# A two-stage state-space scan: new start, seven swapped steps of 32 instead of eight, and a new order of the steps that prepare each chunk

## The chip, the core and the metric

The kernel runs on one core of a Trainium2 chip. The metric is the device time of one execution in microseconds, from the median of the runs. A core has five engines with a queue each: TensorE (PE, its weight loads PEld), VectorE (DVE), ScalarE (ACT), GpSimd (POOL) and SyncE (SP), which here only issues DMAs. Each executes its queue in order and waits on semaphores where an input is not there or an output's buffer is not free.

## The reference

Two layers on x of shape (1, 64, 256, 128) in float32. The first is a pair of bidirectional state-space blocks, one along time (stage 0 below), one along frequency (stage 1); the second is a convolutional LSTM. The change is in the first:

```python
def _mamba(u, p):                       # u: sequences x L x 64, d_inner 128, 16 states
    x, z = split(u @ in_proj)           # after an RMS norm of u
    x = silu(causal_conv4(x) + conv_b)
    dt, B, C = split(x @ x_proj)        # 4 + 16 + 16
    dt = softplus(dt @ dt_proj + dt_b)
    h[t] = exp(dt[t] * A) * h[t-1] + dt[t] * B[t] * x[t]      # A = -exp(A_log)
    y[t] = sum over states(h[t] * C[t]) + x * D
    return (y * silu(z)) @ out_proj
```

Each of the two stages runs it forwards and backwards (d = 0, 1) with weights of its own, adds the input, and multiplies by a closing matrix.

## The kernel before

A chunk is 512 tokens (sequences of one stage laid side by side); a stage has 64 chunks. In a chunk each direction d takes 8 steps, so a chunk has 16 steps, and `Stage.run` goes over S = 0 to 1023 in each stage. What a "turn" S of its loop issues, in this order:

- `times_b(S+1)`: bx times B, 1024 elements a partition, on VectorE in PSUM; for a **swapped** step (S % 32 in `SWAPPED`) on GpSimd instead, on a copy in SBUF.
- `recur(S)`: the scan on VectorE. Every eighth turn (S % 8 == 2) `gate` follows on VectorE, and `skip` on ScalarE.
- `outputs(S-1)`: h times C on GpSimd.
- `inputs(S+2)`: TensorE spreads dt*x over the states into one of three PSUM buffers of bx. The buffer is free when `recur(S-1)` is done.
- `decays(S+2)`: ScalarE makes exp(dt*A), two activations that need the tile rep (dt spread over the partitions by a DMA). For a swapped step ScalarE first copies bx to SBUF and writes the decays into its PSUM place. In turn 5 of a chunk two steps' decays are issued, in turn 6 none.
- the head steps of this turn, then in odd turns `add_up(S-2)` on TensorE, in turns 2 and 3 `close_a`, `close_b` and `keep`, then the head steps of S + 0.5.

The head steps prepare the next chunk. The table `HEAD` gives the turn of each, counted from the start of the chunk before; a turn of 16 or more lies in the chunk itself, a negative one in the chunk before that. The names: `load` (DMA of u), `squares`, `means`, `rms`, `normalise` (xn on GpSimd, then four DMAs), `project_x`, `project_z`, `silus` (two table loads and four activations on ScalarE), `project_bc` (pb on TensorE, the copy bc on ScalarE, a DMA to DRAM called away), `softplus_a` (pv on TensorE, three activations), `softplus_b` (three activations), `softplus_sum` (six matmuls, the copy dt on ScalarE), `dt_away` (four DMAs, called there), `times_x` (dtx on GpSimd), `spread_bc` (the DMAs of B and C from away), `spread_dt` (the DMA of a rep of 512 KB from there; rep n of direction d is for step 8d + n, with seven buffers). The order of the table is the order of each queue, SP's too. The small matmuls of the head (px, pz, pv, pb, po, pm) share one PSUM bank, called mm.

`SECOND` is the table for chunk 0, whose first half is written out in `first`. In stage 0, `first` also makes the weights from raw arrays: `shifts`, `gates`, `dt`, `spreads`, `folds`, `residual`, `closing`, mostly on VectorE. The lines of before that the text names: L322 squares, L332 and L333 rms, L351 normalise_here, L360/L361/L364 projections, L398 pv, L419 softplus_sum, L423 dt, L430 there, L441 pb, L443 bc, L445 away, L451 B and C, L460 rep, L553 inputs, L570 a swapped step's copy, L573/L576 decays, L585 a swapped step's product, L588 times_b, L598 the scan, L611 outputs, L620 add_up, L632 skip, L636 gate.

Of the kernel before, what the change touches and what calls it, by code (L numbers as in the profile page):

```python
# [29 lines left out]
F32 = mybir.dt.float32  # L30
# [6 lines left out]
P = 128  # L37
C = 64
# [8 lines left out]
NTOK = 512  # L47
# [12 lines left out]
RESPOND = 6  # L60
NH = 5
LAG = 2
SWAPPED = (2, 5, 9, 14, 18, 21, 25, 30)
EXP_AND_LN = "natural_log_exp_and_others"
SILU = "silu_and_others"
EDGES = (0, 1, LF - 2, LF - 1)
# [2 lines left out]

HEAD = (  # L70
    (-13, "load"),
    (-8.5, "squares"),
    (-4.5, "means"),
    (-4.5, "rms"),
    (-3, "normalise"),
    (0, "project_x", 0),
    (1.5, "project_z", 0),
    (4, "project_z", 1),
    (5, "project_x", 1),
    (5, "silus"),  # L80
    (7.5, "project_bc", 0),
    (8, "softplus_a", 0),
    (8.5, "softplus_b", 0),
    (8.5, "spread_bc", 0, 0),
    (10.5, "softplus_sum", 0),
    (10.5, "dt_away", 0),
    (11.5, "times_x", 0),
    (12, "spread_bc", 0, 1),
    (12, "spread_dt", 0, 0),
    (12, "spread_dt", 0, 1),  # L90
    (12.5, "project_bc", 1),
    (12.5, "spread_dt", 0, 2),
    (13, "softplus_a", 1),
    (13, "softplus_b", 1),
    (13.5, "spread_dt", 0, 3),
    (14.5, "spread_dt", 0, 4),
    (15, "softplus_sum", 1),
    (15.5, "dt_away", 1),
    (16, "spread_dt", 0, 5),
    (16.5, "spread_dt", 0, 6),  # L100
    (16.5, "spread_dt", 0, 7),
    (17, "spread_dt", 1, 0),
    (17.5, "spread_bc", 1, 0),
    (19, "spread_dt", 1, 1),
    (20.5, "times_x", 1),
    (21, "spread_dt", 1, 2),
    (22, "spread_dt", 1, 3),
    (23, "spread_bc", 1, 1),
    (23, "spread_dt", 1, 4),
    (24, "spread_dt", 1, 5),  # L110
    (26.5, "spread_dt", 1, 6),
    (26.5, "spread_dt", 1, 7),
)


# [3 lines left out]
) + (  # L119
    (14, "softplus_a", 1),  # L120
    (15, "softplus_b", 1),
    (15, "softplus_sum", 1),
    (15, "dt_away", 1),
    (16, "spread_bc", 1, 0),
    (16, "spread_bc", 1, 1),
    (17, "times_x", 1),
)

# [1 line left out]
class Mamba:  # L130
# [3 lines left out]
    def __init__(self, ctx, tc, cols, room, d):  # L134
        nc = tc.nc
        self.nc, self.tc, self.d, self.cols = nc, tc, d, cols
        cp = ctx.enter_context(tc.tile_pool(name="m_const", bufs=1))
        self.ident = cp.tile([P, P], F32, name="ident")
        self.mask = cp.tile([P, 2, NK, DL], F32, name="mask")
        self.sel = cp.tile([P, 2, NK, P], F32, name="sel")  # L140
        self.fold = cp.tile([P, NK, 32], F32, name="fold")
        self.ones = cp.tile([P, P], F32, name="ones")
        self.eps = cp.tile([P, 1], F32, name="eps")
        self.Wbc = cp.tile([P, 4, NBC], F32, name="wbc")
        self.cb, self.dtb, self.dp = (cols[:, 4 * n : 4 * n + 4] for n in range(3))
        self.A = cols[:, 12 : 12 + 4 * NG].rearrange("p (i g) -> p i g", i=4)
        self.G1, self.G2, self.Wz, self.Wdt, self.W2, self.W3 = ([] for _ in range(6))
        for i in range(4):
            for n, t, rows, width in (
                ("g1", self.G1, P, P),  # L150
                ("g2", self.G2, P, P),
                ("wz", self.Wz, C, P),
                ("wdt", self.Wdt, P, P),
                ("w2", self.W2, P, C),
            ):
                t.append(cp.tile([rows, width], F32, name=f"{n}{i}", tag=f"{n}{i}"))
        for i in range(2):
            self.W3.append(cp.tile([P, 2, C], F32, name=f"w3{i}", tag=f"w3{i}"))
        b = cp.tile([C, 2], F32, name="lin_b")
        self.b = b  # L160
        self.lin_b = [b[:, i : i + 1] for i in range(2)]

        room = room.rearrange("p t f -> p (t f)")
        at = 0

        def take(rows, *shape):
            nonlocal at
            n = int(np.prod(shape))
            t = room[0:rows, at : at + n]
            at += n  # L170
            return t

        self.win = take(C, 4, 2 * P + 1).rearrange("p (i n) -> p i n", i=4)
        self.cw = take(C, 4, 4, P).rearrange("p (i k n) -> p i k n", i=4, k=4)
        self.xdt = take(RANK, 8, P).rearrange("p (i n) -> p i n", i=8)
        self.ow = take(C, 4, P).rearrange("p (i n) -> p i n", i=4)
        self.lin = take(C, 4, C).rearrange("p (i n) -> p i n", i=4)


        nc.vector.memset(self.ones, 0.0)  # L180
        for h in range(2):
            own = slice(h * C, (h + 1) * C)
            nc.vector.memset(self.ones[own, own], 1.0 / C)
        nc.vector.memset(self.eps, RMS_EPS)
        for w3 in self.W3:
            nc.vector.memset(w3, 0.0)
        make_identity(nc, self.ident)

    def load(self, first):
        dma, d = self.nc.sync.dma_start, self.d  # L190
# [24 lines left out]
        self.nc.scalar.activation(self.A, self.A, AF.Exp)  # L215
        self.nc.vector.tensor_scalar(self.A, self.A, -1.0, None, ALU.mult)

    def dt(self, i, ps):
        self.nc.tensor.matmul(ps[:, 0:P], lhsT=self.xdt[:, i], rhs=self.xdt[:, 4 + i], start=True, stop=True)
        self.nc.vector.tensor_copy(self.Wdt[i], ps[:, 0:P])  # L220

    def gates(self, i):
        self.nc.vector.tensor_copy(self.Wz[i], self.win[:, i, P : 2 * P])
# [26 lines left out]
        nc.vector.tensor_add(w3[0:C, 0], w3[0:C, 0], self.ident[0:C, 0:C])  # L250
        nc.vector.tensor_copy(w3[C:P, 1], w3[0:C, 0])

    def closing(self, i, ps):
        self.nc.tensor.matmul(ps[:, 0:C], lhsT=self.ow[:, i], rhs=self.lin[:, i], start=True, stop=True)
        self.nc.vector.tensor_copy(self.W2[i], ps[:, 0:C])


class Stage:
# [206 lines left out]
    def head(self, ch):  # L465
        todo = {}
        for slot, name, *args in HEAD if ch else SECOND:
            todo.setdefault(slot, []).append((getattr(self, name), (ch, *args)))
        return todo

    def first(self):


        nc, m = self.nc, self.m
        s, time = 2 * self.stage, self.time
        banks = [self.ps_bx.tile([P, 2, NTOK], F32, name="bx", tag="bx") for _ in range(3)]
        self.load(0)
        if time:
            m.load(True)
        self.squares(0)  # L480
        if time:
            m.shifts(0)
        self.means(0)
        self.rms(0)
        nc.scalar.preload_act_table_set(SILU)
        self.normalise_here()
        if time:
            m.dt(0, self.mm("pw"))
            m.load(False)
        x, z = {}, {}  # L490
        for d in range(2):
            x[d] = self.wk.tile([P, NTOK], F32, name="xs", tag="xs", bufs=3)
            z[d] = self.wk.tile([P, NTOK], F32, name="zs", tag="zs", bufs=4)
            self.at["xs", 0, d], self.at["zs", 0, d] = x[d], z[d]
        self.shifted(banks[0][:, 0], s)
        nc.scalar.activation(x[0], banks[0][:, 0], AF.Silu, bias=m.cb[:, s : s + 1])
        nc.scalar.preload_act_table_set(EXP_AND_LN)
        self.softplus_a(0, 0)
        if time:
            m.decay()  # L500
            m.spreads()
            m.gates(0)
            m.shifts(1)
            m.gates(1)
        self.softplus_b(0, 0)
        self.spare = [banks[0][:, 1]]
        self.project_bc(0, 0)
        self.spread_bc(0, 0, 0)
        self.softplus_sum(0, 0)
        self.dt_away(0, 0)  # L510
        self.times_x(0, 0)
        for n in range(4):
            self.spread_dt(0, 0, n)
            if n == 0:
                self.spread_bc(0, 0, 1)
        if time:
            m.dt(1, self.mm("pw"))
        self.shifted(banks[1][:, 0], s + 1)
        for d in range(2):
            self.gated(banks[1 + d][:, 1], s + d)  # L520
        nc.scalar.preload_act_table_set(SILU)
        nc.scalar.activation(x[1], banks[1][:, 0], AF.Silu, bias=m.cb[:, s + 1 : s + 2])
        for d in range(2):
            nc.scalar.activation(z[d], banks[1 + d][:, 1], AF.Silu)
        nc.scalar.preload_act_table_set(EXP_AND_LN)
        self.spare = [banks[2][:, 0]]
        self.project_bc(0, 1)
        if time:
            m.folds(self.mm("pf"))
            for i in (2, 3):  # L530
                m.shifts(i)
                m.gates(i)
                m.dt(i, self.mm("pw"))
            for n in range(2):
                m.residual(n)
            for i in range(4):
                m.closing(i, self.mm("pc"))

# [15 lines left out]
    def swapped(self, S):  # L556


        return S % 32 in SWAPPED

# [125 lines left out]
    def run(self):  # L686
        nch = NCH
        last = 16 * nch
        silu = next(slot for slot, name, *_ in HEAD if name == "silus")
        steps = {}  # L690
# [1 line left out]
            for slot, todo in self.head(ch).items():  # L692
                steps.setdefault(16 * (ch - 1) + slot, []).extend(todo)
        self.first()
        for S in range(int(min(steps)), last + LAG + 4):
            if 0 <= S + 1 < last:
                self.times_b(S + 1)
            if 0 <= S < last:
# [24 lines left out]
            if not self.time and S > 16:  # L723
# [5 lines left out]
                n = S // 16 - 1  # L729
# [533 lines left out]
```

## Time and profile before

| | |
|---|---|
| median of 3 runs | 7323.06 us (7319.82 to 7334.2) |
| the profiled execution | 7325.76 us, span 7324.0 us |
| first to last scan of stage 0 | 48.69 to 3319.25 us |
| first to last scan of stage 1 | 3356.72 to 6629.66 us |
| the LSTM and what prepares it | the rest of the span |
| mean granted TensorE clock | 0.975 |

In the profile an instruction has the line of its kernel, the engine, the operation, and the tiles out<-in. A group's columns are the busy time, the mean of one in ns, and the idle time of its engine just before them with what ended it. In a timeline a line has its start and length in us, and in brackets the idle time before it. Times are from the span's start; the median of the runs and the profiled execution are different executions.

### The profile page before, as it was taken

Reading aid. Unit: us, or ns where it says so; the run is one execution under the profiler, and the core shown is the slowest. Engines: PE = TensorE matmul, PEld = TensorE weight load, DVE = VectorE, ACT = ScalarE, POOL = GpSimd, SP = SyncE. Lnnn points to the kernel's source line nnn. Section 1 sums busy time; section 2 is a strip of 40 time slices with the busy share of each in tenths; the row PEclk is TensorE's granted clock in tenths of the full one; section 3 lists DMA queues with packets and bytes.
Section 4 is the critical chain, followed back from the end, with each engine's and each line's share of the span. In section 5 each row is a group of like instructions: output and inputs, shape, how many; then the busy total and the mean of one; then the engine's idle time right before and its main releaser. Section 6 shows DMA issues by size and latency. Waiting matters only on the chain. (4 is left out here: it accounts for less than half of the span.)

```text
span 7324.0 us, 86482 instructions
## 1 busy us (share of the span) xinstructions
PE 6510.4 (89%) x25104; PEld 2254.8 (31%) x25104; DVE 6924.8 (95%) x4684; ACT 6119.2 (84%) x11092; POOL 6703.3 (92%) x3410
## 2 busy tenths in 40 slices
PE   8888888888888888887898898888888888888999
PEld 2222222222222222222222222222222222226887
DVE  7999999999999999997999999999999999996887
ACT  7888889888898888987999999988998989983333
POOL 6999999999999999997999999999999999995554
PEclk9999999999999999999999999999999999999999
DMA  7888888888888888886888888878888788882000
GB/s 171 206 206 208 199 210 204 205 207 205 210 203 209 206 204 207 204 210 159 208 211 209 210 215 200 208 197 202 206 201 204 199 209 198 205 202 62 15 15 17
DMA packets 505887, 1359.47 MB, mean 186 GB/s; under 512 B 72772, under 2 KB 129732, under 8 KB 505416
## 3 DMA queue, kind: packets, MB, share of 16 engines
q1 hardware_dynamic: 505416, 1353.93, 74.6%
q8 instruction: 205, 3.36, 0.2%
q14 instruction: 266, 2.18, 0.1%
HBM read 1228.34 MB, written 92.27 MB: 180 GB/s over the span
## 5 line engine op out<-in xcount | busy, mean ns | idle before, releaser
L611 POOL TENSOR_TENSOR h<-h,C 128x1024 f32<-128x1024 f32 x2048 | 4797.5, 2366 | 32.4 <-DVE h L598 22.0
L598 DVE TENSOR_TENSOR_SCAN h<-dA,bx 128x1024 f32<-128x1024 f32 x1536 | 3443.8, 2269 | 0.0
L553 PE MATMUL bx<-dtx,sel 64*128 64x512 f32 x8192 | 2578.7, 653 | 364.8 <-DVE h L598 362.5
L588 DVE TENSOR_TENSOR bx<-bx,B 128x1024 f32<-128x1024 f32 x1536 | 1863.7, 1213 | 178.8 <-PE bx L553 178.2
L576 ACT ACTIVATE dA<-rep,cols 128x510 f32<-128x510 f32 (+1 forms) x3072 | 2021.7, 710 | 11.3 <-DMA rep<-there 11.3
L585 POOL TENSOR_TENSOR dA<-dA,B 128x1024 f32<-128x1024 f32 x512 | 1205.9, 2355 | 161.9 <-ACT dA L570 155.8
L553 PEld LDWEIGHTS bx<-dtx,sel 64*128 64x128 f32 x8192 | 733.3, 190 | 1888.1 <-issue 1070.5
L620 PE MATMUL y<-h,fold 128*32 128x512 f32 x8192 | 1239.5, 618 | 12.6 <-POOL h L611 10.9
L598 DVE TENSOR_TENSOR_SCAN h<-bx,dA 128x1024 f32<-128x1024 f32 x512 | 1167.9, 2281 | 15.4 <-POOL dA L585 15.4
L570 ACT COPY dA<-bx 128x1024 f32<-128x1024 f32 x512 | 518.5, 1013 | 352.7 <-PE bx L553 338.0
L576 ACT ACTIVATE bx<-rep,cols 128x510 f32<-128x510 f32 (+1 forms) x1024 | 705.5, 689 | 33.7 <-ACT bx L573 0.4
L398 PE MATMUL pv<-xs,wdt 128*128 128x512 f32 x512 | 341.2, 753 | 261.5 <-ACT bc L443 167.5
L620 PEld LDWEIGHTS y<-h,fold 128*32 128x32 f32 x8192 | 188.5, 109 | 933.5 <-issue 504.0
L435 POOL TENSOR_TENSOR dtx<-dt,xs 128x512 f32<-128x512 f32 x256 | 327.6, 1280 | 54.2 <-ACT dt L423 33.7
L364 PE MATMUL pz<-unp,wz 64*128 64x512 f32 x504 | 283.5, 642 | 91.0 <-ACT X L669 54.0
L360 PE MATMUL px<-unp,g 128*128 128x512 f32 x504 | 283.8, 644 | 9.5 <-DMA unp<-xn 7.0
L419 PE MATMUL pv<-e,ident 128*128 128x512 f32 x512 | 288.1, 645 | 3.4 <-ACT e L402 3.4
L441 PE MATMUL pb<-xs,wbc 128*32 128x512 f32 x504 | 260.9, 599 | 15.6 <-ACT made L809 15.6
L419 PE MATMUL pv<-w,ident 128*128 128x512 f32 x512 | 262.6, 594 | 6.1 <-ACT w L411 6.1
L419 PE MATMUL pv<-lw,ident 128*128 128x512 f32 x512 | 262.3, 594 | 0.0
L361 PE MATMUL px<-unp,g 128*128 128x512 f32 x504 | 257.8, 592 | 0.0
L1150 POOL TENSOR_TENSOR y<-v,X 128x512 f32<-128x512 f32 x32 | 40.6, 1270 | 230.7 <-DVE v L1148 230.7
(206 smaller groups left out, 7066.0 us busy)
## 6 DMA issues: line engine op xcount, KB each, us to landing
rep<-there SPq DMA_DIRECT2D x2048, 512.0 KB, 7.8
B<-away SPq DMA_DIRECT2D x256, 256.0 KB, 8.9
there<-dt SPq DMA_DIRECT2D x1024, 64.0 KB, 3.3
C<-away SPq DMA_DIRECT2D x256, 256.0 KB, 3.4
unp<-xn SPq DMA_DIRECT2D x504, 64.0 KB, 3.3
away<-bc SPq DMA_DIRECT2D x256, 64.0 KB, 4.1
u<-in_x SPq DMA_DIRECT2D x128, 64.0 KB, 8.9
out<-y SPq DMA_DIRECT2D x32, 256.0 KB, 2.0
```

What stands on the lines that cost most here:

```text
L360: nc.tensor.matmul(self.seqs(px), lhsT=m.G1[i], rhs=self.unp[:, :, first : first + L], start=True, stop=False)
L398: nc.tensor.matmul(pv, lhsT=m.Wdt[i], rhs=self.at["xs", ch, d], start=True, stop=True)
L419: nc.tensor.matmul(pv, lhsT=self.m.ident, rhs=t, start=False, stop=n == len(parts) - 1, skip_group_check=True)
L435: self.nc.gpsimd.tensor_mul(dtx, self.at["dt", d], self.at["xs", ch, d])
L553: self.nc.tensor.matmul(bx[:, j], lhsT=self.m.sel[rows, r, k], rhs=dtx[rows], start=True, stop=True)
L570: nc.scalar.copy(dA.rearrange("p j n l -> p j (n l)"), bx)
L576: nc.scalar.activation(dA[:, j, :, live], self.seqs(rep[:, j])[:, :, live], AF.Exp, scale=m.A[:, i, g : g + 1])
L585: self.nc.gpsimd.tensor_mul(bx, bx, b)
L588: self.nc.vector.tensor_mul(bx, bx, b)
L598: self.nc.vector.tensor_tensor_scan(h.rearrange("p j n -> p (j n)")[:, step], dA[:, step], bx[:, step], 0.0, ALU.mult, ALU.add,)
L611: self.nc.gpsimd.tensor_mul(h, h, self.at["C", ch, d].unsqueeze(1).to_broadcast([P, 2, NTOK]))
L620: nc.tensor.matmul(y[32 * r : 32 * r + 32], lhsT=m.fold[:, k], rhs=hs[r % 2][:, r // 2], start=False, stop=k == NK - 1, skip_group_check=True,
```

## The change

It has four parts.

- **SWAPPED** has seven steps of 32 instead of eight.
- **HEAD** has new turns for most steps. project_x(0), project_z(1), normalise, squares, means, both B and C, softplus_sum(0), dt_away, times_x(0) and most reps move; `dt_away` of the second direction goes from turn 15.5 to 18. **SECOND**, for chunk 0, asks for B and C of direction 1 before its softplus_sum and dt_away, which move from turn 15 to 16.
- **first** asks for the second chunk's u at once, behind the weights' DMAs, makes all weights ahead of `softplus_b` of chunk 0 in buffers that were idle, and the constructor asks for the table set of exp and ln.
- `dt` and `closing` make their four matrices in one PSUM bank and copy them at once.

```diff
-SWAPPED = (2, 5, 9, 14, 18, 21, 25, 30)
+SWAPPED = (2, 5, 9, 13, 19, 25, 29)
 HEAD = (
     (-13, "load"),
-    (-8.5, "squares"),
-    (-4.5, "means"),
+    (-8, "squares"),
+    (-5, "means"),
     (-4.5, "rms"),
-    (-3, "normalise"),
-    (0, "project_x", 0),
+    (-3.5, "normalise"),
+    (0.5, "project_x", 0),
     (1.5, "project_z", 0),
-    (4, "project_z", 1),
+    (4.5, "project_z", 1),
     (5, "project_x", 1),
     (5, "silus"),
     (7.5, "project_bc", 0),
     (8, "softplus_a", 0),
     (8.5, "softplus_b", 0),
-    (8.5, "spread_bc", 0, 0),
-    (10.5, "softplus_sum", 0),
-    (10.5, "dt_away", 0),
-    (11.5, "times_x", 0),
-    (12, "spread_bc", 0, 1),
+    (9, "spread_bc", 0, 1),
+    (10, "softplus_sum", 0),
+    (11, "dt_away", 0),
+    (12, "spread_bc", 0, 0),
     (12, "spread_dt", 0, 0),
-    (12, "spread_dt", 0, 1),
+    (12, "times_x", 0),
     (12.5, "project_bc", 1),
-    (12.5, "spread_dt", 0, 2),
+    (12.5, "spread_dt", 0, 1),
     (13, "softplus_a", 1),
-    (13, "softplus_b", 1),
-    (13.5, "spread_dt", 0, 3),
-    (14.5, "spread_dt", 0, 4),
+    (13, "spread_dt", 0, 2),
+    (13.5, "softplus_b", 1),
+    (14, "spread_dt", 0, 3),
     (15, "softplus_sum", 1),
-    (15.5, "dt_away", 1),
+    (15.5, "spread_dt", 0, 4),
     (16, "spread_dt", 0, 5),
     (16.5, "spread_dt", 0, 6),
-    (16.5, "spread_dt", 0, 7),
-    (17, "spread_dt", 1, 0),
-    (17.5, "spread_bc", 1, 0),
+    (18, "dt_away", 1),
+    (18, "spread_dt", 0, 7),
+    (19, "spread_dt", 1, 0),
     (19, "spread_dt", 1, 1),
     (20.5, "times_x", 1),
-    (21, "spread_dt", 1, 2),
-    (22, "spread_dt", 1, 3),
-    (23, "spread_bc", 1, 1),
+    (20.5, "spread_bc", 1, 0),
+    (21, "spread_bc", 1, 1),
+    (23, "spread_dt", 1, 2),
+    (23, "spread_dt", 1, 3),
     (23, "spread_dt", 1, 4),
-    (24, "spread_dt", 1, 5),
-    (26.5, "spread_dt", 1, 6),
-    (26.5, "spread_dt", 1, 7),
+    (24.5, "spread_dt", 1, 5),
+    (24.5, "spread_dt", 1, 6),
+    (27, "spread_dt", 1, 7),
 )
...
-    (15, "softplus_sum", 1),
-    (15, "dt_away", 1),
-    (16, "spread_bc", 1, 0),
-    (16, "spread_bc", 1, 1),
+    (16, "softplus_sum", 1),
+    (16, "dt_away", 1),
+    (14, "spread_bc", 1, 0),
+    (15, "spread_bc", 1, 1),
...
+        nc.scalar.preload_act_table_set(EXP_AND_LN)
...
-    def dt(self, i, ps):
-        self.nc.tensor.matmul(ps[:, 0:P], lhsT=self.xdt[:, i], rhs=self.xdt[:, 4 + i], start=True, stop=True)
-        self.nc.vector.tensor_copy(self.Wdt[i], ps[:, 0:P])
+    def dt(self, ps):
+        ps = ps.rearrange("p (i n) -> p i n", i=4)
+        for i in range(4):
+            self.nc.tensor.matmul(ps[:, i], lhsT=self.xdt[:, i], rhs=self.xdt[:, 4 + i], start=True, stop=True)
+        self.nc.vector.tensor_copy(self.wdt, ps)
...
         self.means(0)
         self.rms(0)
+        if time:
+            m.load(False)
+            m.decay()
+        self.load(1)
         nc.scalar.preload_act_table_set(SILU)
         self.normalise_here()
         if time:
-            m.dt(0, self.mm("pw"))
-            m.load(False)
...
+            m.dt(banks[2][:, 1])
...
         self.softplus_a(0, 0)
         if time:
-            m.decay()
             m.spreads()
-            m.gates(0)
+            m.folds(banks[1][:, 1])
+            m.closing(banks[2][:, 0])
             m.shifts(1)
-            m.gates(1)
+            for i in range(2):
+                m.gates(i)
+                m.residual(i)
+            for i in (2, 3):
+                m.shifts(i)
+                m.gates(i)
         self.softplus_b(0, 0)
...
-            m.dt(1, self.mm("pw"))
...
-            m.folds(self.mm("pf"))
-            for i in (2, 3):
-                m.shifts(i)
-                m.gates(i)
-                m.dt(i, self.mm("pw"))
-            for n in range(2):
-                m.residual(n)
-            for i in range(4):
-                m.closing(i, self.mm("pc"))
```

`closing` is changed as `dt` is. The loop of `run` starts one turn before the first head step, and `head` leaves out the load of chunk 1.

## The prediction

> **What bounds it now.** I read the page's busy row first, then the busy time by stretches, then VectorE's groups by shape in the first stage, then the timelines around VectorE's idle spots.
>
> ```profile
> PE 6510.4 (89%) x25104; PEld 2254.8 (31%) x25104; DVE 6924.8 (95%) x4684; ACT 6119.2 (84%) x11092; POOL 6703.3 (92%) x3410
> ```
> ```profile
> 1000.00:3000.00 2000.00, 1773.28 (x6648) 507.81 (x6648) 1951.74 (x1175) 1783.51 (x3173) 1944.95 (x901) 0.97 0.83 206
> ```
> The columns of the second are PE, PEld, DVE, ACT and POOL busy, then the TensorE clock, the DMA share and GB/s. VectorE is busy 97.6% of a steady stretch and GpSimd 97.2%. VectorE's own work in stage 0:
>
> ```profile
> L598 DVE TENSOR_TENSOR_SCAN h<-dA,bx 128x1024 f32<-128x1024 f32 x756 | 1695.0, 2269 | 0.0
> L588 DVE TENSOR_TENSOR bx<-bx,B 128x1024 f32<-128x1024 f32 x756 | 917.2, 1213 | 74.2 <-PE bx L553 73.9
> L598 DVE TENSOR_TENSOR_SCAN h<-bx,dA 128x1024 f32<-128x1024 f32 x253 | 577.1, 2281 | 0.3 <-POOL dA L585 0.3
> L636 DVE TENSOR_TENSOR yz<-y,zs 128x512 f32<-128x512 f32 x126 | 83.7, 664 | 0.0
> ```
> VectorE waits for TensorE's bx (73.9 us) and for GpSimd once: GpSimd runs behind but never holds it up. So VectorE is the bound, plus its waits for bx. In its timeline a scan starts 2.19 us before the next instruction, a multiplication 1.11 to 1.17 (I take 1.13), a gate 0.58. Over 32 steps (two chunks, 8 of them swapped) that is 32 x 2.19 + 24 x 1.13 + 4 x 0.58 = 99.5 us. The first scans of a stage start at 48.69 and 3356.72, its last at 3319.25 and 6629.66: 102.3 and 102.4 us for 32 steps. The remainder is idle. Summing the idle by turn of the loop (modulo 32, 30 periods of each stage), it sits in six turns, means for stage 0 / stage 1: turn 2 0.34/0.50, turn 9 0/0.26, turn 10 0.96/0.43, turn 18 0.30/0.39, turn 25 0/0.26, turn 26 0.78/0.55. Turns 10 and 26 are not smooth: 0 in some periods, 1.0 to 1.6 in the others. Why, TensorE's timeline and the stretches show:
>
> ```profile
> 998.83 1.13 PE L553 MATMUL bx<-dtx,sel 64*128 64x512 f32 x4 [0.34 <-DVE h L598]
> 1001.79 2.06 PE L398 MATMUL pv<-xs,wdt 128*128 128x512 f32 x2 [1.83 <-ACT bc L443]
> 1003.78 1.84 PE L553 MATMUL bx<-dtx,sel 64*128 64x512 f32 x4
> ```
> ```profile
> 1005.67 1.23 DVE L588 TENSOR_TENSOR bx<-bx,B 128x1024 f32<-128x1024 f32 x1 [1.33 <-PE bx L553]
> ```
> ```profile
> 998.40:1001.80 3.40, 1.22 (x6) 0.32 (x5) 3.40 (x3) 3.29 (x7) 3.33 (x2) 1.00 0.04 12
> 1001.80:1005.20 3.40, 3.40 (x6) 0.98 (x6) 2.53 (x2) 2.88 (x7) 3.40 (x3) 0.50 0.55 159
> ```
> ScalarE copies bc late (behind silus and a swapped step's copy), TensorE idles 1.83 us before softplus_a, its clock then falls to 0.50, pv and the next bx take 1.84 to 2.06 instead of 1.13, and VectorE waits 1.33. From 3400 to 4400 us the same wait is 0.96, the clock stays 1.00, and turns 10 and 26 have no stall.
>
> [...]
>
> **Part 1, the start of stage 0.**
>
> ```profile
> 30.35 0.57 ACT L443 COPY bc<-bx 32x512 f32<-32x512 f32 x1
> 40.80 0.42 ACT L322 ACTIVATE sq<-u 128x256 f32<-128x256 f32 x1 [9.88 <-DMA u<-in_x]
> ```
> ScalarE's queue stands 9.88 us at the second chunk's squares, because that load is issued at 31.91, behind the reps; decays(0) is queued behind. Issued after the weights (at about 7.8) it lands by some 13 (5.2 median of these loads). Then squares follow bc at 31. Before, from squares (40.80) to the first scan (48.69) are 7.9 us; kept, the first scan comes at 39, less 1 for the matmul of dt(1) (0.48 and its wait of 0.68) that leaves the path. The table set asked for at the start removes two loads of 1.28 from the chain squares, means, rms and hides the third behind the first DMA: 2.6 to 3.8 us. Given back: folds and closing on TensorE ahead of project_bc (1.1 + 4 x 0.68), and Exp of A 0.25. I count nothing net for these two together (bounds -3 to +2). VectorE's weights, 31.18 to 39.8, now lie in 10.7 to 28, where it idled 8.36; by 38 all are done. One copy of 128x512 out of PSUM (0.66, as the gate) replaces four of 0.28: nothing, off the path. First scan 48.7 to 38: **-11** (bounds -7 to -15). The reps 4 and 5 no longer stand behind the second dt_away in SP's queue; ScalarE waited 4.2 us for reps between 60 and 72, VectorE 0.94 there: **-1** (0 to -3). Stage 1's start gets the same queue order without the loads: **-1** (+2 to -3).
>
> **Part 2, seven swapped steps.** Steps 14, 18, 30 become 13, 19, 29; 21 is dropped. VectorE gets one multiplication more per period: +1.13. GpSimd loses 2.35, ScalarE a copy of 1.01 and its wait (1.10 at 1036.75): both off the path. What comes back:
> - Turn 18: step 18 is no longer swapped, so multiplication 18 lies between, and bx(19) has 1.13 more; the idle there (0.33 nearly always) goes: -0.30/-0.39. In turn 19 the same squeeze arises for bx(20), but the gate's 0.58 is in between and no close_a yet: no new idle (bound +0.2).
> - Turn 26: in the odd chunk VectorE, and with it bx(26), is later by 1.13 - 0.45 = 0.7, ScalarE earlier by 0.1 to 0.6 (keep waits for close_b, behind add_up, so not the whole 1.0). The TensorE wait falls from 1.83 to 0.6-1.0, where the clock stayed up: -0.78/-0.55 in turn 26, and part of turn 25.
> - Even chunks keep 2, 5, 9 and the same order of TensorE and ScalarE between turns 0 and 10: turns 2 and 10 stay. 13 for 14: GpSimd's product of step 13 would end near 1015, its scan starts at 1016.2; no gain, no loss.
>
> Sum: stage 0 +1.13 - 0.30 - 0.78 = +0.05; stage 1 +1.13 - 0.39 - 0.55 - 0.1 = +0.1. With a residue in turn 26, **+0.12 a period, 64 periods: +8**. Bounds: nothing comes back, +72; the half clock also leaves turn 10, -60. [...]
>
> **Part 3, the other moves.** project_x(0), project_z(1): half a turn later with nothing of TensorE or ScalarE in between: 0. squares behind softplus_a: 0.41 on ScalarE later; softplus_sum has TensorE work before it: 0, without that cover +0.4 a chunk. softplus_sum(0) ahead of skip: the dt copy (0.58) goes before skip (0.69), so add_up of turn 11 starts some 0.4 later, behind means that now fills it: 0 (up to +0.2). means and rms earlier, times_x(0) half a turn later on GpSimd (1.28): dtx is wanted two turns on, 0.
> SP's queue: dt_away(1) moves from 15.5 to 18, behind reps 4 to 6, which need no wait; rep 1 stands behind bc's away (lands near -3.6 us from the chunk's first scan, used at -2.1), reps 2 to 4 behind xn (slack about 1.5). there(1) lands some 10 us after issue instead of 4 to 5, and rep 8, which waits for it, at about 15.8 instead of 14.6, used at 17.3: slack 2.7 to 1.5 us. B(0) changes places with C(0): wanted 4 us after landing. So 0, but thin: each chunk in which rep 8 is late by 1 us costs up to 1 us, as silus and bc stand behind it on ScalarE.
>
> **Sum.** 7325.8 (profiled execution: span 7324.0 and 1.8 around it) - 11 - 1 - 1 + 8 = 7320.8. The median of the runs shown is 2.7 below that execution: about 7318.
>
> **Rivals.**
> - *The multiplication is not paid back* (slower). Turn 26 keeps its stall: rep 8 late, or ScalarE held at keep, so that TensorE still idles. It decides if that wait stays above about 1.2 us (no half clock at 0.96, in most chunks at 1.83). Cost 1.13 - 0.35 = 0.78 x 64 = 50, less 13: **7360**; with turn 18's gain lost too, 7382. For it: the thin slack of rep 8, and 128 chunks of new SP order. Against: ScalarE drops a copy just there.
> - *The half clock goes in even chunks too* (faster). With the odd chunk undisturbed, turn 10 stalls less often: 0.96/0.43 halved and stage 1's turn 9 and 25 smaller: -0.6 x 64 = -38, and -13: **7272**. For it: two chunks without the half clock took 100.3 us. Against: the 1.83 before turn 10 is not touched by any edit.
> - *The early load does not start the loop*: rep 0 lands late, or TensorE at half clock holds the chain. Start gain 4 instead of 13: **7327**.
>
> **Numbers.** A measurement of this kernel can tell about 0.2%, 14.6 us, from no change: below 7308.4 is faster, above 7337.7 slower. The likeliest, a loop about even and a shorter start (with the last rival in it, 0.44), spans 7300 to 7338: faster 0.08, same 0.36. Not paid back or new waits 0.34, all slower; half clock gone 0.22, faster 0.20, same 0.02. Together faster 0.28, same 0.38, slower 0.34. The range takes in 7272 and, for the thin SP slack, 7375.
>
> **What would show it.** Right: first scan near 38, no wait for u on ScalarE; 7 of 32 steps on GpSimd, VectorE over 98% busy; turn 18 and 26 free of idle, TensorE's wait before the odd pv below 1.0; turn 10 as before. Wrong: ScalarE waiting for rep, B or C landing late, VectorE waiting in turns 12 to 14 or 19 to 20, the half clock in odd chunks.

## The result and the profile after

The changed kernel takes 7336.33 us (median of 20 runs, 7325.09 to 7352.9) against 7322.89 us for the kernel before on the same chip (20 runs, 7313.98 to 7334.2): ratio 1.0020, 95% interval 1.0013 to 1.0027. It is some 13 us slower, a small loss that the runs can tell from none.

The profiled execution took 7342.42 us, 6 above that median; its span is 7340.6. Set against the profiled execution before, stretch by stretch:

| stretch | before, us | after, us | difference |
|---|---|---|---|
| start to the first scan of stage 0 | 48.69 | 37.43 | -11.3 |
| stage 0, first to last scan | 3270.6 | 3284.4 | +13.8 |
| to the first scan of stage 1 | 37.5 | 42.9 | +5.4 |
| stage 1, first to last scan | 3272.9 | 3278.5 | +5.6 |
| to the end of the span | 694.3 | 697.4 | +3.1 |

The third and the last row can't be put down to the change. Over the 18 profiles of this document the way from stage 0 to stage 1 takes 37.4 to 42.9 us and the end 694.3 to 697.7. Where the way takes 37.4 to 37.5, the granted clock is 0.50 for 3.6 to 4.1 us of it, elsewhere for 6.8 to 20.5 (the mean of this stretch is 0.95 before, 0.80 after). Two kernels below whose code for it is that of before take 42.4 and 42.6.

The start came as forecast. ScalarE's timeline of the changed kernel shows the copy of bc and the second chunk's squares back to back, with no wait for u between them; before, the same squares stood 9.88 us at their load:

```profile
31.35 0.57 ACT L449 COPY bc<-bx 32x512 f32<-32x512 f32 x1
31.83 0.41 ACT L328 ACTIVATE sq<-u 128x256 f32<-128x256 f32 x1
```

The loops lost it again. The page's busy row, and the stretch from 1000 to 3000 us (PE, PEld, DVE, ACT, POOL busy; then clock, DMA share, GB/s), after:

```profile
PE 6526.5 (89%) x25104; PEld 2262.2 (31%) x25104; DVE 6984.0 (95%) x4742; ACT 5985.1 (82%) x10834; POOL 6554.7 (89%) x3346
```
```profile
1000.00:3000.00 2000.00, 1769.92 (x6624) 506.18 (x6624) 1960.30 (x1188) 1731.88 (x3077) 1888.58 (x877) 0.98 0.83 205
```

GpSimd and ScalarE are relieved (1945 to 1889, 1784 to 1732), VectorE is busier (1952 to 1960), as one multiplication more in 32 steps must make it. Where it still waits, VectorE's groups by shape in stage 0 show, over the stretch used before:

```profile
L602 DVE TENSOR_TENSOR_SCAN h<-dA,bx 128x1024 f32<-128x1024 f32 x784 | 1766.2, 2273 | 10.6 <-PE y L624 10.0 <-DVE h L602 0.5
L592 DVE TENSOR_TENSOR bx<-bx,B 128x1024 f32<-128x1024 f32 x785 | 950.5, 1211 | 49.9 <-PE bx L557 48.8 <-DMA B<-away 0.6
L602 DVE TENSOR_TENSOR_SCAN h<-bx,dA 128x1024 f32<-128x1024 f32 x220 | 501.8, 2281 | 0.0
```

The multiplications' wait for bx fell from 74.2 to 49.9 us, but a new wait of 10.6 stands before the scans. The next table takes 28 periods of 32 steps (two chunks) from the middle of each stage and gives means of one period, stage 0 / stage 1; VectorE's idle was also summed by turn:

| | period | idle in it | the rest, VectorE's work |
|---|---|---|---|
| before | 102.27 / 102.23 | 2.48 / 2.43 | 99.79 / 99.80 |
| after | 102.65 / 102.53 | 1.95 / 1.78 | 100.70 / 100.75 |

Turns 10, 18, 25 and 26, which held 2.13 us of the idle in stage 0 and 1.66 in stage 1, are down to 0 and 0.35. Turn 2, 0.34 and 0.49 before, is at 1.54 and 0.88, and turn 1 is new with 0.35 and 0.17. In stage 0 that is +0.91 of work, -0.31 and -0.83 at turns 18 and 26, -0.99 at turn 10, and +1.55 at turns 1 and 2: +0.33 of the +0.38 measured.

TensorE's timeline shows where the new stall comes from. First the inputs of turn 31 in the kernel before, then those of turns 30 and 31, and what follows them, in the changed kernel:

```profile
970.36 1.13 PE L553 MATMUL bx<-dtx,sel 64*128 64x512 f32 x4 [1.02 <-DVE h L598]
```

```profile
1059.15 1.13 PE L557 MATMUL bx<-dtx,sel 64*128 64x512 f32 x4
1062.46 2.08 PE L557 MATMUL bx<-dtx,sel 64*128 64x512 f32 x4 [2.18 <-DVE h L602]
1064.47 1.69 PE L425 MATMUL pv<-e,ident 128*128 128x512 f32 x2
1065.99 1.02 PE L425 MATMUL pv<-w,ident 128*128 128x512 f32 x2
```

and VectorE's timeline, ten us later:

```profile
1072.95 1.23 DVE L592 TENSOR_TENSOR bx<-bx,B 128x1024 f32<-128x1024 f32 x1 [1.58 <-PE bx L557]
```

Before, step 30 was swapped, so VectorE had no multiplication 30, scan 30 ended early, and TensorE waited 1.02 us there for a free bx (0.15 to 1.24 in the 28 periods of stage 0). With 29 in its place the multiplication of step 30 is VectorE's again, the scan ends later, and TensorE stands 2.18 us in each of them. Its clock then halves just as it has inputs(33) and the whole softplus_sum(1) to do (1.69 us for a pair that takes 1.13 at full clock), and everything queued behind, bx(35) of turn 2 last, is late.

In the traces of before and after the recorded granted clock is 1.00 or 0.50. Its changes lie on one grid of 3.413 us, in each trace through the whole span and to within 0.001 us, and a stretch at 0.50 lasts 3.41 us (52 of 79 before, 71 of 83 after) or, but for the one at the end of each trace, two to four times that. Below, a "window" is one step of this grid, "half clock" a stretch at 0.50, and a "fall" its start. The lines show two windows, one before and one after a fall, twice:

```profile
239.62:243.03 3.41, 1.23 (x8) 0.33 (x4) 3.41 (x3) 3.31 (x9) 3.41 (x2) 1.00 0.57 142
243.03:246.44 3.41, 3.41 (x6) 1.25 (x5) 3.41 (x3) 1.28 (x3) 3.41 (x3) 0.50 0.96 252
...
1058.82:1062.23 3.41, 1.33 (x8) 0.33 (x4) 3.41 (x3) 3.31 (x7) 3.41 (x3) 1.00 1.00 232
1062.23:1065.64 3.41, 3.18 (x6) 1.19 (x7) 3.41 (x4) 2.24 (x5) 3.41 (x2) 0.50 0.82 220
```

Two things are to be seen. TensorE was busy 1.23 and 1.33 of 3.41 us, then its clock was 0.50. And 1062.23 - 243.03 = 819.20 us is 8 times 102.40: from the first of these falls to the last the half clock comes back every 102.40 us, thirty windows, at step 30 of each period.

### The profile page after: what moved, and what is told of

Same layout as the page of the kernel before. It is cut to its first block, busy times and chain, and to the rows that moved or that the text cites. A ratio compares the mean times of both kernels' runs of the same rounds, so it can differ in the third digit from the quotient of the medians.

```text
span 7340.6 us, 86535 instructions
## 1 busy us (share of the span) xinstructions
PE 6526.5 (89%) x25104; PEld 2262.2 (31%) x25104; DVE 6984.0 (95%) x4742; ACT 5985.1 (82%) x10834; POOL 6554.7 (89%) x3346
## 4 chain that ended last, share of the span: by engine, by line
PE 22%; ACT 14%; DVE 9%; issue 7%; DMA 1%; POOL 1%; SPq 0%; DVEq 0%; POOLq 0%; ACTq 0%
PE cv L1031 6%; DVE h L602 5%; PE bx L557 5%; ACT dA L580 3%; PE pv L425 3%; DVE bx L592 3%; ACT bx L580 2%; PE y L624 2%; ACT dA L574 2%; PE px L366 1%; DMA rep<-there 1%; PE px L367 1%; ACT X L673 1%; PE pg L1087 1%; ACT L391 1%
## 5 line engine op out<-in xcount | busy, mean ns | idle before, releaser
L615 POOL TENSOR_TENSOR h<-h,C 128x1024 f32<-128x1024 f32 x2048 | 4787.4, 2365 | 52.2 <-DVE h L602 49.9
L602 DVE TENSOR_TENSOR_SCAN h<-dA,bx 128x1024 f32<-128x1024 f32 x1600 | 3602.2, 2273 | 15.8 <-PE y L624 14.3
L557 PE MATMUL bx<-dtx,sel 64*128 64x512 f32 x8192 | 2520.2, 649 | 432.4 <-DVE h L602 424.9
L580 ACT ACTIVATE dA<-rep,cols 128x510 f32<-128x510 f32 (+1 forms) x3200 | 2105.0, 710 | 69.7 <-DMA rep<-there 64.6
L592 DVE TENSOR_TENSOR bx<-bx,B 128x1024 f32<-128x1024 f32 x1600 | 1938.2, 1211 | 137.5 <-PE bx L557 135.9
L589 POOL TENSOR_TENSOR dA<-dA,B 128x1024 f32<-128x1024 f32 x448 | 1054.5, 2354 | 321.8 <-ACT dA L574 233.1
L602 DVE TENSOR_TENSOR_SCAN h<-bx,dA 128x1024 f32<-128x1024 f32 x448 | 1021.8, 2281 | 5.8 <-POOL dA L589 5.7
L580 ACT ACTIVATE bx<-rep,cols 128x510 f32<-128x510 f32 (+1 forms) x896 | 617.4, 689 | 30.4 <-ACT bx L577 1.1
L574 ACT COPY dA<-bx 128x1024 f32<-128x1024 f32 x448 | 453.6, 1013 | 200.5 <-PE bx L557 199.2
L404 PE MATMUL pv<-xs,wdt 128*128 128x512 f32 x512 | 293.9, 656 | 186.2 <-ACT bc L449 135.5
L429 ACT COPY dt<-pv 128x512 f32<-128x512 f32 x256 | 148.6, 580 | 244.9 <-PE pv L425 244.6
```

Of the source, the lines that this page charges most:

```text
L557: self.nc.tensor.matmul(bx[:, j], lhsT=self.m.sel[rows, r, k], rhs=dtx[rows], start=True, stop=True)
L574: nc.scalar.copy(dA.rearrange("p j n l -> p j (n l)"), bx)
L580: nc.scalar.activation(dA[:, j, :, live], self.seqs(rep[:, j])[:, :, live], AF.Exp, scale=m.A[:, i, g : g + 1])
L589: self.nc.gpsimd.tensor_mul(bx, bx, b)
L592: self.nc.vector.tensor_mul(bx, bx, b)
L602: self.nc.vector.tensor_tensor_scan(h.rearrange("p j n -> p (j n)")[:, step], dA[:, step], bx[:, step], 0.0, ALU.mult, ALU.add,)
```

## The experiments

There were three theories at first. **A**: swap 29 for 30 costs the time, by the half clock at step 30. **B**: the loop hangs on the clock's windows, and any list of swaps gets a period of about 102.4 us. **C**: the new step list costs the time. All ratios are set against the kernel before in the same series of runs; periods are stage 0, then stage 1.

### The change taken apart

**The new start alone**: the changed kernel with HEAD and SECOND of before (not shown) and the old swaps:

```diff
-SWAPPED = (2, 5, 9, 13, 19, 25, 29)
+SWAPPED = (2, 5, 9, 14, 18, 21, 25, 30)
...
```

> The new start alone (early load of the second chunk, early table, weights made in VectorE's idle stretch), with the old step list and the old eight swaps. All theories: the first scan at 37 to 38 us as in the changed kernel, no wait anywhere in the loop altered, so 10 to 13 us less than the kernel before, ratio 0.9982 to 0.9987. If the clock's windows hold the loop to a period of thirty of them (theory B), part of this can be lost by a shift against them: down to 0.9995.

7313.16 us, 0.9987 (0.9980 to 0.9993): the start is worth 10 us, and no more is lost than B allowed. In its profile the first scan comes at 31.93, earlier than expected, and the first 64 scans take 3.6 us longer than before.

**The new swaps alone**, in the kernel before:

```diff
-SWAPPED = (2, 5, 9, 14, 18, 21, 25, 30)
+SWAPPED = (2, 5, 9, 13, 19, 25, 29)
```

> The kernel before with only the seven new swaps (2, 5, 9, 13, 19, 25, 29). Theory A (29 in place of 30 makes TensorE wait over 2 us at turn 30, its clock halves there, and turn 2 stalls 1.6 us): period per 32 steps 102.6 to 102.9 us, the wait ahead of turn 2 at 1.5, 20 to 30 us slower than before, 1.003 to 1.004. Theory B (the loop hangs on the clock's windows, thirty to a period, and every list of swaps gets some idle spot): period 102.4 to 102.6, 1.001 to 1.003. Theory C (the new step list, not the swaps, costs the time): within 5 us of before, below 1.0007.

7338.97 us, 1.0020 (1.0012 to 1.0029), periods 102.37 and 102.20, turn 2 at 1.12 and 0.36. The swaps cost 15 us without the new step list: C falls as the main cause. The ratio is B's, not A's; both periods lie just under B's 102.4. In its profile the loops hold only 7.6 us of the loss; 4.3 stand in the way into stage 1 and 3.0 at the end, which vary as much where nothing was changed.

**The new step list alone** (HEAD and SECOND of the change in the kernel before):

> The kernel before with only the new step list (HEAD and SECOND), the old eight swaps and the old start. Theory A: within 5 us of before, 0.9993 to 1.0007, the half clock still at turns 8 and 24. Theory B: the same. Theory C (the step list costs: the third dt spread lands late, ScalarE waits): 10 to 25 us slower, 1.0014 to 1.0034.

7329.61 us, 1.0008 (1.0002 to 1.0015): 6 us, just over what A and B allowed. VectorE waits 0.2 us at turns 14 and 30, where it did not before; the changed kernel, which swaps 13 and 29, has no such wait. The three parts add up to -10 + 15 + 6 = +11, against 13 measured; as these waits are not in the changed kernel, the agreement is partly luck.

**30 for 29** in the changed kernel:

```diff
-SWAPPED = (2, 5, 9, 13, 19, 25, 29)
+SWAPPED = (2, 5, 9, 13, 19, 25, 30)
```

> The changed kernel with one number turned back: swap 30 in place of 29. Theory A: TensorE's wait at turn 30 is 1.0 us again, no half clock there, turn 2 waits 0.3 to 0.5 as before; period 101.0 to 101.4 us, 60 to 80 us faster than the kernel before, 0.989 to 0.992. Theory B: the half clock goes to another wait of TensorE (turn 8 of even chunks, 1.8 us), period 102.2 to 102.6, so 0.9985 to 1.0010. Theory C: as the changed kernel, 1.001 to 1.003.

7316.62 us, 0.9992 (0.9984 to 1.0001): 20 us below the changed kernel, so this one number decides between a small loss and none. The loops of its profile are 9.9 and 8.2 us shorter. Turn 2 is back at 0.33 and no half clock starts at step 30, as A said, although TensorE still waits 1.54 us there and not 1.0. But A's 60 to 80 us did not come: the half clock now starts at steps 8, 9, 14 and 24 (33 falls in the 56 periods), and both periods are 102.16. The size is B's again.

ScalarE's wait for rep 2, the other new wait of the changed kernel, does not explain the stall of turn 2: over the span it is still 41 us here, against 56 in the changed kernel, and turn 2 is at 0.33.

### Filling TensorE's wait

**Theory D** says how the lock of B comes about. In the middle of stage 0 of the kernel before, the windows just ahead of a fall have 1.23 to 1.66 us of TensorE's work, and 98% of the others over 2.1; D puts the falls down to this lack of work, and the lack to the two waits ahead of pv. Then work without use, put into those waits, must free the loop. A matmul of zeros onto y, which changes no value, goes ahead of the first pv of each chunk but chunk 0:

```diff
+        self.none = cp.tile([P, P], F32, name="none")
...
+        nc.gpsimd.memset(self.none, 0.0)
...
+    def fill(self):
+        m = self.m
+        rhs = m.sel[:, 0].rearrange("p k n -> p (k n)")
+        self.nc.tensor.matmul(self.y, lhsT=m.none, rhs=rhs, start=False, stop=False, skip_group_check=True)
...
         pv = self.mm("pv")
+        if ch and d == 0:
+            self.fill()
```

**In the kernel before:**

> The kernel before with one more matmul: zeros onto y (about 1.1 us), issued ahead of each first pv matmul, where TensorE waits 1.83 us for its bank. It changes no value. Theory D (the loop is held near 102.4 us [...]): no half clock at turns 8 and 24, turns 10 and 26 wait less than 0.4, period 100.3 to 100.9 us, 80 to 120 us faster, 0.983 to 0.989. Theory B in its strong form (some other wait takes over): period stays 102.1 to 102.5, 0.998 to 1.002. Rival: the added matmul only makes pv late, 1.0 to 1.01.

7240.03 us, 0.9888 (0.9873 to 0.9902): **83 us faster, by 126 added matmuls**. TensorE's timeline and the stretch from 1000 to 3000 us of this kernel:

```profile
1687.50 1.13 PE L562 MATMUL bx<-dtx,sel 64*128 64x512 f32 x4 [0.34 <-DVE h L607]
1688.56 1.13 PE L397 MATMUL y<-sel,none 128*128 128x512 f32 x2
1690.46 1.13 PE L407 MATMUL pv<-xs,wdt 128*128 128x512 f32 x2 [0.77 <-ACT bc L452]
1691.51 1.13 PE L562 MATMUL bx<-dtx,sel 64*128 64x512 f32 x4
```
```profile
1000.00:3000.00 2000.00, 1806.62 (x6838) 521.70 (x6837) 1979.28 (x1192) 1807.01 (x3218) 1972.50 (x915) 1.00 0.86 209
```

pv still comes when bc has been copied, not later: the fill took 1.06 of the 1.83 us. pv and bx behind it take 1.13 where they took 1.84 to 2.06, the clock is 1.00, turns 10 and 26 are free, and the periods are 100.55 and 101.17 (the second just above the 100.9 expected). With the waits filled no fall is left in the 56 periods, as D says; B in its strong form, that another wait must take over, falls.

**With the new start:**

> The new start with the old step list and old swaps, and the same matmul of zeros ahead of each first pv. Theory D: 10 us below the kernel before with the matmul, 90 to 130 us faster than before, 0.982 to 0.988. Theory B strong: 0.997 to 1.001.

7227.16 us, 0.9869 (0.9852 to 0.9885): the best kernel here, 96 us below before in its series and 109 below the changed one in another.

**In the changed kernel with 30 for 29:**

> The changed kernel with 30 for 29 and the matmul of zeros ahead of each first pv. Theory D: only turns 2 (0.33), 17 (0.3) and 30 (0.2) still wait, period 101.3 to 101.7 us since seven swaps leave VectorE 0.8 us more work than eight; 40 to 60 us faster than before, 0.992 to 0.995, so 50 us behind the eight swaps with the same matmul. Theory B strong: 102.1 to 102.4, 0.998 to 1.0.

7265.88 us, 0.9921 (0.9906 to 0.9936), periods 101.21 and 101.52. As forecast: with the clock up, seven swaps fall behind eight.

**In the changed kernel, with a third fill** ahead of the inputs of step 31:

```diff
             if 0 <= S + 2 < last:
+                if S % 32 == 31 and S > 0:
+                    self.fill()
                 self.inputs(S + 2)
```

> The changed kernel with the matmul of zeros ahead of each first pv and a third one ahead of the inputs of step 31, where 29 in place of 30 opened the wait of 2.18 us. Theory A with D: no half clock at steps 30 and 31, turn 2 waits 0.3 to 0.5 instead of 1.54, period 101.0 to 101.6, 45 to 85 us faster than before, 0.988 to 0.994. If the wait itself and not the clock behind it stalls turn 2: turn 2 stays near 1.5, period 102.2 to 102.6, 0.999 to 1.002.

7253.08 us, 0.9904 (0.9889 to 0.9918). At turn 31 TensorE still waits for scan 30, with 1.06 of the 2.18 us filled, and turn 2 waits 0.33: it was the clock behind the wait, not the wait, that stalled it. With its wait filled, the swap of 29 is no worse than that of 30 in the kernel above (7265.88).

**The same fill elsewhere**, at steps 5 and 21 of the kernel before (`if S % 16 == 5 and S > 0`):

> The kernel before with the same two matmuls of zeros a period, put ahead of the inputs of steps 5 and 21, where TensorE works without a break. Theory D: the waits ahead of pv stay 1.83 us, half clock at turns 8 and 24 as before, period 102.1 to 102.6, 0.998 to 1.003. If a changed order or more work for TensorE anywhere were what helped: 0.985 to 0.993.

7445.36 us, 1.0169 (1.0154 to 1.0185). The half clock stays at steps 8, 9, 24 and 25, as D says, and so more work for TensorE is no cure by itself. The price was missed: each fill there delays the bx behind it, VectorE waits 0.55 more at turns 7 and 23 and 0.19 at 9 and 25, and stage 0's period is 104.35.

**A quarter of the fill** (128 of 512 columns), to see how much work in the wait is enough:

> The kernel before with the matmul of zeros ahead of each first pv cut to 128 of 512 columns (about 0.27 us in place of 1.06). Theory D [...] some half clock stays (5 to 20 windows a stage against 39 and 24), period 100.7 to 101.7, 0.989 to 0.996; [...] If the bound were a whole idle stretch of fixed length that any work breaks: no half clock at all, 0.987 to 0.990.

7278.33 us, 0.9947 (0.9932 to 0.9962), 6 falls in stage 0 and 18 in stage 1, periods 100.76 and 102.14, the second above the 101.7 expected. A quarter ends most of the falls of stage 0 (39 before) and a quarter of those of stage 1 (24), so not any work in the wait is enough. Where the line lies was not shown: windows ahead of a fall in stage 0 had 1.55 to 1.92 us of work here, 1.23 to 1.66 before, and the others here 1.88 and more (matmul ends are modelled, so neither figure is sharp; in the kernel of 7265.88 us windows of 1.75 had no fall behind them).

### Eight swaps with 19 in place of 18

With the clock up, what is left in stage 0 are turns 2 and 18. In the best kernel, 18 and 21 were moved to 19 and 22, then 2 and 5 to 3 and 6 too:

```diff
-SWAPPED = (2, 5, 9, 14, 18, 21, 25, 30)
+SWAPPED = (2, 5, 9, 14, 19, 22, 25, 30)
```

> The new start, the old step list, the full matmul of zeros ahead of each first pv, and eight swaps with 18 and 21 moved to 19 and 22. As in the changed kernel turn 18 no longer waits for bx (0.44 us a period), and no multiplication is added: period 100.0 in stage 0, 100.6 in stage 1, 25 us less than with the old swaps, 0.9825 to 0.9850 of before. GpSimd's own work (32 products of 2.37, 8 of 2.36, 4 of 1.28 us) is 99.8 us a period: if it binds, period 100.4 and no gain over the old swaps, 0.986 to 0.988.

> As the one with 19 and 22, and 2 and 5 moved to 3 and 6 likewise: turn 2's 0.39 us go too, period 99.9 in stage 0 (GpSimd's 99.8 is near), 100.2 in stage 1, 0.978 to 0.983. If GpSimd binds: no better than the one with 19 and 22.

7307.01 us (0.9979, 0.9973 to 0.9986) and 7385.17 us (1.0089, 1.0072 to 1.0106): 80 and 158 us above the 7227.16 of the old places. Turn 18 is free, but GpSimd, without slack, is now late with the products. VectorE's and GpSimd's timelines of the first of them:

```profile
1742.54 2.29 DVE L611 TENSOR_TENSOR_SCAN h<-bx,dA 128x1024 f32<-128x1024 f32 x1 [0.45 <-POOL dA L598]
...
1752.57 2.29 DVE L611 TENSOR_TENSOR_SCAN h<-bx,dA 128x1024 f32<-128x1024 f32 x1 [0.64 <-POOL dA L598]
```
```profile
1731.98 6.99 POOL L624 TENSOR_TENSOR h<-h,C 128x1024 f32<-128x1024 f32 x3
1738.93 1.26 POOL L450 TENSOR_TENSOR dtx<-dt,xs 128x512 f32<-128x512 f32 x1
1740.15 2.35 POOL L598 TENSOR_TENSOR dA<-dA,B 128x1024 f32<-128x1024 f32 x1
```

The product of step 22 stands behind three outputs and times_x. I had a bound for GpSimd's sum over a period (99.8 us), not for its queue between two swaps. So 18 can go to 19 in this loop where 21 is dropped, as the change did; whether some other eight would do was not tried.

### What the windows do to a sum

It was then open how a multiplication added and stalls removed could both count for so little. **Theory E:** while a half clock is about, the stalls it makes fill the period up to near a whole number of windows. The same multiplication was added twice, by leaving out swap 21, without and with the fill:

```diff
-SWAPPED = (2, 5, 9, 14, 18, 21, 25, 30)
+SWAPPED = (2, 5, 9, 14, 18, 25, 30)
```

> The kernel before with swap 21 left out and nothing else: one multiplication of 1.13 us more for VectorE in 32 steps. Theory E (while a half clock is about, the stalls fill the period up to about 102.4 us, thirty windows): the stalls at turns 10 and 26 shrink by most of it, period 102.2 to 102.6, 0 to 20 us slower, 1.000 to 1.003. Plain sum: 64 times 1.13, less what turns 25 and 26 give back in any case (0.1 to 0.3), 50 to 72 us slower, 1.007 to 1.010.

> The same swap left out of the kernel with the matmul of zeros ahead of each first pv (7240 us). Theory E: with no half clock the multiplication costs its full price: period 101.5 in stage 0 and 102.0 in stage 1, 50 to 72 us above that kernel, so 7290 to 7312, 0.9955 to 0.9985 of before. If the multiplication is cheap wherever it is: 7240 to 7260, 0.989 to 0.9915.

Without the fill 7337.52 us against 7326.12, 1.0012 (1.0003 to 1.0020); with it 7294.98, 55 above the 7240.03 of the same kernel with eight swaps (measured in an earlier series, where before was 3 us lower). VectorE's work grew alike, by 0.92 and 1.05 us a period in stage 0. But without the fill its idle fell from 2.48 to 1.18, and with it from 0.93 to 0.79 only. (The profiled execution of the first is 13 us below its median, so its idle is on the low side.) **The price of one and the same edit is 9 to 11 us with the half clock about, and some 50 without** (46 by the two ratios, 55 by the medians).

That fits theory E, but does not show it. Without the fill the edit also shortens TensorE's wait ahead of the odd chunk's pv, from 1.83 to 0.80 us in stage 0 and from 2.12 to 0.80 in stage 1 (medians), and no fall follows it. One such wait:

```profile
1050.46 1.12 PE L398 MATMUL pv<-xs,wdt 128*128 128x512 f32 x2 [0.81 <-ACT bc L443]
```

Turn 26 thereby loses its whole stall, 0.83 of the 0.92 added in stage 0; in stage 1 turns 25 and 26 lose 0.85 of 0.96. The kernel with the fill has no such stall at turn 26 to lose. A plain sum that has this term gives 0.1 us a period, 6 us in all, so that no lock to the windows is needed for the small price.

Last, the changed kernel with only one of its two kinds of wait filled: step 31 alone, then pv alone.

> The changed kernel with the matmul of zeros only ahead of the inputs of step 31. Theory E: the half clock leaves step 30 and turns up at steps 8, 9 and 14 as with swap 30, turn 2 waits 0.34 again; period 102.1 to 102.4, 7310 to 7325 us, 0.998 to 1.0005. If step 30 was the whole trouble: period 101.0 to 101.4, 7255 to 7275, 0.9905 to 0.9935.

> The changed kernel with the matmul of zeros only ahead of each first pv, step 31's wait left open. Theory E: half clock at step 30 nearly every period, turn 2 at about 1.4, period 102.4 to 102.6 in both stages, 7325 to 7340 us, 1.000 to 1.0025. If step 30's wait does harm only along with those ahead of pv: period below 101.6, 0.990 to 0.995.

With step 31 filled 7295.82 us, 0.9953 (0.9938 to 0.9968): the half clock moved to steps 8, 9 and 14 (30 falls) and turn 2 is at 0.33, as E said, but the periods are 101.59 and 102.08, shorter than its 102.1 to 102.4. E fails here. In stage 0 five of the 13 spacings between falls are 303.79 us, 89 windows to three periods; the others differ, so it is no lasting lock. TensorE's timeline has the filled wait and the full clock behind it:

```profile
1055.10 1.12 PE L403 MATMUL y<-sel,none 128*128 128x512 f32 x2
1057.35 1.13 PE L564 MATMUL bx<-dtx,sel 64*128 64x512 f32 x4 [1.13 <-DVE h L609]
1058.41 1.12 PE L432 MATMUL pv<-e,ident 128*128 128x512 f32 x2
```

With pv filled 7324.48 us, 0.9999 (0.9992 to 1.0006), stage 0's period 102.40, with a half clock at step 30 in each of the 28 periods. Stage 1 has 17 falls and a period of 102.16, under E's 102.4, and the time is just under E's 7325. Four half-clock windows of stage 0, in the columns used above:

```profile
140.39:143.80 3.41, 3.29 (x6) 1.30 (x7) 3.41 (x3) 2.13 (x5) 3.41 (x2) 0.50 0.82 185
242.79:246.20 3.41, 3.22 (x6) 1.23 (x7) 3.41 (x4) 2.19 (x5) 3.41 (x2) 0.50 0.78 217
1676.39:1679.80 3.41, 3.16 (x6) 1.17 (x7) 3.41 (x4) 2.25 (x5) 3.41 (x2) 0.50 0.73 196
3212.38:3215.79 3.41, 3.17 (x6) 1.18 (x7) 3.41 (x4) 2.25 (x5) 3.41 (x2) 0.50 0.75 167
```

From 140.39 to 3212.38 are 30 periods of 102.40 us, each with one fall. VectorE's work there is 100.67 us; the stall at turns 1 and 2, 1.73, is what is missing to 102.40. That is the lock, shown for this stage; what holds the stall at just that size was not shown.

## Why the prediction was wrong

What failed is the step that put the moved swaps at no gain and no loss. The prediction gave 7318 us and most of its chance to "not slower"; 7336.33 is 18 above, inside its range, on the side of "same" by its own bound of 7337.7, but the interval of the ratio lies above 1. Point by point, with the profiled executions:

- **The start, -11:** right, -11.3 in the profile, and 10 us for the whole start by itself. The two small items beside it can't be seen: the first 64 scans of stage 0 went from 209.5 to 209.1, those of stage 1 from 211.2 to 206.1, but over the 18 profiles these take 206.1 to 213.6. The way into stage 1 took 5.4 longer, where +2 to -3 was allowed, with 17.1 us at half clock in it instead of 3.6; as said above, it varies as much without this change.
- **The multiplication, +1.13:** 0.91 and 0.95 in the accounting; sized right.
- **Turns 18 and 26 go:** right, by the mechanism named. Both are 0 to 0.05, and TensorE's wait ahead of the odd chunk's pv went from 1.83 to 1.00 in stage 0, at the upper end of the 0.6 to 1.0 forecast, and from 2.12 to 1.28 in stage 1. With pv filled in the changed kernel turn 18 stays free, so its gain has nothing to do with the clock.
- **"Even chunks keep ... turns 2 and 10 stay. 13 for 14: ... no gain, no loss":** the failed step. Turn 10 went from 0.99 to 0 in stage 0, and turns 1 and 2 from 0.34 to 1.89. I had looked at what the moved swaps do to GpSimd and ScalarE, and not at what VectorE's later scan does to TensorE, which waits for scan 30 with inputs(33). I did not even name 29 for 30, and so put it at nothing. Turned back, it is 20 us, more than the whole loss; with that wait alone filled the changed kernel takes 7295.82.
- **The sum, +0.12 a period:** +0.38 and +0.30, 22 us for 64 periods instead of 8. In stage 0 its own terms came out at +0.91, -0.31 and -0.83, that is -0.23; what it lacked is +1.55 at turns 1 and 2 and -0.99 at turn 10. That falls move from one wait to another had no term in it either: from step 30 they went to steps 8, 9, 14 and 24 with 30 for 29, and to 8, 9 and 14 with step 31 filled. Of the rivals, "half clock gone" (7272) was right on the price of the half clock: the changed kernel with all three waits filled takes 7253. It left turn 2 out, and that turn 10 emptied brought no gain, since the falls went to step 30. That the forecast came within 18 us owes something to luck: two terms that it lacked cancel in part.
- **SP's thin slack:** mostly right to leave at 0. Where it bit was not rep 8 but rep 2: ScalarE's wait for reps went from 11.3 to 64.6 us over the span, 56 of it for the rep of step 2. The new step list cost 6 us by itself, but not by this: with the old swaps ScalarE waits only 8.0 us for reps. What rep 2 costs in the changed kernel was not separated.

## What to carry to other kernels

Where TensorE waits a few us in each period of a loop, look at its work per clock window before counting any stall as a cost: in this kernel the clock was at 0.50 after windows with 1.23 to 1.66 of 3.41 us of work (stage 0 of before), and with pv filled the changed kernel's stage 0 locked to 102.40 us, thirty windows. Removing one such wait moved the falls to others (from step 30 to 8, 9 and 14), so ask of an edit which waits it lengthens and shortens, and where the falls go then. A matmul of zeros in each such wait, placed where it delays nothing, is the first thing to try: here two in 32 steps left no fall in the 56 periods of the kernel before, and three left two in those of the changed kernel. When a swap moves by one step, follow not only the engines that trade the work but the next one that waits for the result.

## What was not expected of the hardware

- Work without use pays: two matmuls of zeros in 32 steps, 1.06 us each, took 83 us off 7323. The weights of these matmuls are all zero, and yet with them the mean granted clock went from 0.975 to 0.995.
- The half clock came after windows in which TensorE still worked 1.23 to 1.66 of 3.41 us (stage 0 of before), with a wait of only 1.83 us, or 2.18 in the changed kernel; a matmul of zeros of a quarter of the size took the 39 falls of stage 0 to 6.
- The lock is exact where it holds: in the changed kernel with pv filled each of the 28 periods in the middle of stage 0 has one fall, 102.40 us after the last.
